# Scores and weighted sums of a pair's two heads issued in turns, one head on each half of the matmul array

## Chip, cores, metric

One core of a Trainium2 chip. The metric is device time in microseconds (us) of one execution of the whole program, lower is better. With one core there is no second die to compare, so a run is called fast if it lies within 1.5% of the fastest of its kernel.

PE is TensorE's matmul side, PEld its weight loads, DVE VectorE, ACT ScalarE, POOL GpSimd. "L157" is line 157 of the kernel in question; lines differ between kernels. A record is one line of the trace; an fp32 product leaves two (the eight score products of two heads are 16 records). The granted clock is the share of TensorE's full clock in the trace's clock records: there it is 1.0 or 0.5 and changes only on a grid of 3.413 us (788 records before, all but the last of whole multiples); records of 128x512 (L122 before) start 429 ns apart at 1.0 and 853 at 0.5 (medians). One step of this grid is called a stretch below.

## The reference, cut to what matters

Two images of 512 channels and 64 x 64 pixels go through four residual layers. Three of the four have attention over 8 heads of 64 channels, against 256 keys or features:

```python
# layer 0: 256 pooled keys and a 3 x 3 window in one softmax, plus learned window weights
attn_pool = jnp.einsum('bhnd,bhpd->bhnp', q_scaled, _l2norm(k_pool))
attn = jax.nn.softmax(jnp.concatenate([attn_local, attn_pool], axis=-1), axis=-1)
x_pool = jnp.einsum('bhnp,bhpd->bhnd', a_pool, v_pool)
# layer 1: 256 sampled keys
sim = jnp.einsum('bhid,bhjd->bhij', qh, kh)
out = jnp.einsum('bhij,bhjd->bhid', jax.nn.softmax(sim, axis=-1), vh)
# layer 3: 256 random features of keys and queries
data_dash = jnp.einsum('bhnd,md->bhnm', data * normalizer, proj)
context = jnp.einsum('bhnm,bhnd->bhmd', kp, v)
out = jnp.einsum('bhnm,bhmd->bhnd', qp, context) / denom[..., None]
```

Layer 2 (a choice of max pools) is not touched.

## The kernel before: what the change and the argument touch

Two heads share the 128 partitions of a channel chunk, so a head's scores contract over 64 rows and a head's weighted sum fills 64 output columns: `64*128` and `128*64` in the trace, where a full product (L122) is `128*128`, so half of the rows and half of the columns. A block is 512 tokens, a "pair" below is two heads of one block: 32 pairs per stage and image ("batch").

```python
def scores(self, pS, q, keys, h):
    lo = h * HD
    for t in range(NT):
        self.nc.tensor.matmul(pS[:, t, :], q[lo:lo + HD, t * P:(t + 1) * P],
                              keys[lo:lo + HD, :], start=True, stop=True)

def weighted(self, psO, prob, vals, h, sp, pp):
    pTs = []
    for k2 in range(2):
        pT = sp.tile([P, TB], F32, name="pT", bufs=2)
        # ... four transposes of prob into PSUM, copied to pT by ACT (k2 = 0) or DVE (k2 = 1)
    for k2 in range(2):
        nc.tensor.matmul(psO[h * HD:(h + 1) * HD, :], vals[:, k2, :], pTs[k2],
                         start=(k2 == 0), stop=(k2 == 1))

# layer 0, attend(blk); prepare(blk + 1) is issued in turn with it, a step at each yield
for h in range(2):
    pS = pps.tile([P, NT, NK], F32, name="pS")          # two such score tiles in PSUM
    self.scores(pS, qs, own["kp"], h)
    # ... maxima (DVE), yield, exp (ACT), normalisation (DVE), yield
    self.weighted(psO, prob, own["vp"][:, :, h * HD:(h + 1) * HD], h, wp, pp)
    yield
# ... nine taps: matmul(ps, taps[:, k, :], lt), 18 rows; product with vx on DVE into prod
#     (3 buffers); sum over taps on POOL; the final sum on DVE

# layer 3, context: one head g after the other
    self.scores(pS, Y[:, g // 2, blk * TB:(blk + 1) * TB], proj, g % 2)
    # ... four exp on ACT into kf, + 1e-4 on DVE, four matmuls va^T kf into ps
```

Layer 1's attention, layer 3's keys (scores and a maximum only) and layer 3's queries have the same loop over `h`. The build puts the instructions of each engine into an order of its own within what the dependences allow.

## Time and profile before

| | us |
|---|---|
| median of 4 runs | 10126.5 (10124.7 to 10127.7) |
| layer 0 attention, one batch | 1889 |
| layer 1 attention | 767 |
| layer 3 keys / context / queries | 320 / 362 / 850 |
| everything else in a batch | about 870 |

The stage lengths in this document are read from each trace between the same marker instructions (for instance the first score of layer 1 and the first pooling instruction of layer 2); they hold the seams between stages too, and so differ by some us from the windows in the prediction. Batch 1 is given where nothing else is said. A batch takes half of the span, so what a stage loses counts twice in the time.

### The profile page before, as it was taken

The numbers are of one execution on the slowest core, as the hardware profiler recorded it, in microseconds if no ns is written. First come the engines' busy times: TensorE is split into PE (matmuls) and PEld (weight loads), VectorE is DVE, ScalarE is ACT, GpSimd is POOL, SyncE is SP. The second block draws the span as 40 slices with busy tenths as digits, with TensorE's granted clock in tenths as the row PEclk, the third lists the DMA queues.
The fourth block names the chain that finished last, engine by engine and source line by source line (L and its number), as shares of the span: only waits on it lengthen the run. The fifth ranks groups of instructions, "written<-read, shape, count | busy, mean of one in ns | idle before, by whom it ended". The sixth has DMA issues, their size and how long they took to land. (4 is left out here: it accounts for less than half of the span.)

```text
span 10124.4 us, 68201 instructions
## 1 busy us (share of the span) xinstructions
PE 8632.9 (85%) x25390; PEld 4059.3 (40%) x25390; DVE 4276.9 (42%) x7503; ACT 2048.9 (20%) x4873; POOL 1093.5 (11%) x1190
## 2 busy tenths in 40 slices
PE   7989898988786699888889898989888876998887
PEld 3333333344333255544443333333443332555443
DVE  3444444425334922244434444444352359222343
ACT  1111111105222101222211111111142221022222
POOL 0222222200000000000002222222000000100000
PEclk9878888889887889977788887887898888899877
DMA  1000000000000000100000000000000000000000
GB/s 46 0 4 0 3 0 0 0 22 1 0 0 9 1 0 5 38 9 13 9 15 0 4 0 4 0 0 0 22 1 0 0 9 1 0 5 5 13 9 13
DMA packets 34324, 66.76 MB, mean 7 GB/s; under 512 B 2532, under 2 KB 15076, under 8 KB 32970
## 3 DMA queue, kind: packets, MB, share of 16 engines
q1 hardware_dynamic: 33994, 62.40, 1.8%
q8 instruction: 202, 3.31, 0.1%
q14 instruction: 128, 1.05, 0.0%
HBM read 45.62 MB, written 16.78 MB: 6 GB/s over the span
## 5 line engine op out<-in xcount | busy, mean ns | idle before, releaser
L122 PE MATMUL mm<-big,w 128*128 128x512 f32 x2560 | 1371.4, 682 | 0.0
L122 PEld LDWEIGHTS mm<-big,w 128*128 128x128 f32 x2560 | 532.6, 221 | 727.4 <-issue 639.9
L449 POOL TENSOR_TENSOR acc<-acc,prod 128x512 f32<-128x512 f32 x512 | 663.4, 1296 | 1441.3 <-DVE prod L444 1392.6
L442 PE MATMUL mm<-lt,taps 18*128 18x512 f32 x1152 | 761.2, 804 | 0.0
L166 PE MATMUL mm<-cst,prob 128*128 128x128 f32 x2048 | 429.7, 370 | 273.0 <-DVE prob L524 247.9
L388 PE MATMUL mm<-prod,cst 128*18 128x512 f32 x1152 | 648.5, 713 | 0.0
L169 DVE COPY pT<-mm 128x512 f32<-128x512 f32 x384 | 265.5, 691 | 787.4 <-PE mm L166 787.4
L166 PEld LDWEIGHTS mm<-cst,prob 128*128 128x128 f32 x2048 | 342.7, 194 | 511.3 <-issue 508.7
L154 PE MATMUL pS<-proj,big 64*128 64x256 f32 x2048 | 459.4, 444 | 98.5 <-ACT big L772 49.9
L444 DVE TENSOR_TENSOR prod<-vx,mm 128x512 f32<-128x512 f32 x512 | 351.9, 687 | 443.9 <-PE mm L442 356.6
L384 DVE TENSOR_TENSOR prod<-qs,kx 128x512 f32<-128x512 f32 x576 | 443.2, 800 | 195.6 <-PE mm L388 194.3
L713 PE MATMUL acc<-big,dg 128*128 128x512 f32 x768 | 369.0, 639 | 136.3 <-DVE big L681 71.4
L171 ACT COPY pT<-mm 128x512 f32<-128x512 f32 x384 | 224.8, 585 | 1000.8 <-PE mm L166 1000.8
L681 DVE TENSOR_TENSOR big<-big 128x3968 f32<-128x3968 f32 x96 | 410.4, 4286 | 21.2 <-PE acc L713 18.3
L442 PEld LDWEIGHTS mm<-lt,taps 18*128 18x128 f32 x1152 | 241.4, 232 | 424.9 <-issue 245.9
L154 PEld LDWEIGHTS pS<-proj,big 64*128 64x128 f32 x2048 | 307.1, 211 | 242.4 <-ACT big L772 103.7
L166 PE MATMUL mm<-cst,qf 128*128 128x128 f32 x1024 | 207.1, 354 | 219.0 <-DVE qf L884 219.0
L420 ACT ACTIVATE prob<-pS,nm 128x256 f32<-128x256 f32 x512 | 235.8, 473 | 630.9 <-DVE nm L415 625.7
L173 PE MATMUL psO<-pT,ctxm 128*64 128x512 f32 x512 | 334.2, 788 | 33.0 <-ACT pT L171 33.0
L173 PE MATMUL psO<-pT,vals 128*64 128x512 f32 x512 | 361.7, 800 | 0.0
L516 DVE TENSOR_REDUCE nm<-pS 128x4 f32<-128x1024 f32 x128 | 150.7, 1219 | 480.8 <-PE pS L154 480.8
L154 PE MATMUL pS<-proj,q 64*128 64x256 f32 x1024 | 280.2, 522 | 53.4 <-ACT q L863 53.4
(267 smaller groups left out, 11377.5 us busy)
## 6 DMA issues: line engine op xcount, KB each, us to landing
big<-in_x SPq DMA_DIRECT2D x8, 2048.0 KB, 8.3
out<-big SPq DMA_DIRECT2D x16, 1024.0 KB, 4.1
w<-in_W_kv SPq DMA_DIRECT2D x16, 256.0 KB, 3.8
big<-in_w_kv SPq DMA_DIRECT2D x2, 2048.0 KB, 7.8
w_sr<-in_W_sr SPq DMA_DIRECT2D x2, 1024.0 KB
w<-in_W_q SPq DMA_DIRECT2D x8, 256.0 KB, 3.0
w_proj<-in_W_proj SPq DMA_DIRECT2D x2, 1024.0 KB, 5.4
big<-in_w_out SPq DMA_DIRECT2D x2, 1024.0 KB
```

The costliest lines, as they stand in the source:

```text
L122: self.nc.tensor.matmul(ps, w[:, kc, :], X[:, kc, blk * TB:(blk + 1) * TB], start=(kc == 0), stop=(kc == KC - 1))
L154: self.nc.tensor.matmul(pS[:, t, :], q[lo:lo + HD, t * P:(t + 1) * P], keys[lo:lo + HD, :], start=True, stop=True)
L166: nc.tensor.transpose(ps[:, t * P:(t + 1) * P], prob[:, t, k2 * P:(k2 + 1) * P], self.ident)
L169: nc.vector.tensor_copy(pT, ps)
L173: nc.tensor.matmul(psO[h * HD:(h + 1) * HD, :], vals[:, k2, :], pTs[k2], start=(k2 == 0), stop=(k2 == 1))
L384: nc.vector.tensor_tensor(pr.rearrange("p (y x) -> p y x", x=W), qs.rearrange("p (y x) -> p y x", x=W), kx[:, dy:dy + 8, dx:dx + W], ALU.mult)
L388: nc.tensor.matmul(ps[:18, :], self.cst[:, C_TAP + 8 - k:C_TAP + 26 - k], pr, start=(k == 0), stop=(k == 8))
L442: nc.tensor.matmul(ps, taps[:, k, :], lt, start=True, stop=True)
L444: nc.vector.tensor_tensor(pr.rearrange("p (y x) -> p y x", x=W), vx[:, dy:dy + 8, dx:dx + W], ps.rearrange("p (y x) -> p y x", x=W), ALU.mult)
L449: nc.gpsimd.tensor_tensor(acc, acc, pr, ALU.add)
L681: nc.vector.tensor_tensor(o, a, b, ALU.max)
L713: nc.tensor.matmul(accs[b], dg, p2[:, b * TB:(b + 1) * TB], start=(j == 1), stop=(j == 6))
```

## The change

Its intent: two matmuls that use different halves of the array can run at the same time. (In the trace before, the sixteen records of L606, which alternate between the column halves, take 1.95 us, and the sixteen of L833, which all have the same columns, 3.67.) So both heads' score tiles are taken at once and their matmuls alternate, and the weighted sums wait until both heads are transposed and then alternate too. What the diff comes to, without the comments that it also drops:

```diff
-    def scores(self, pS, q, keys, h):
-        lo = h * HD
-        for t in range(NT):
-            self.nc.tensor.matmul(pS[:, t, :], ...)
+    def scores(self, q, keys, pps):
+        pS = [pps.tile([P, NT, NK], F32, name="pS") for _ in range(2)]
+        for t in range(NT):
+            for h in range(2):
+                lo = h * HD
+                self.nc.tensor.matmul(pS[h][:, t, :], q[lo:lo + HD, t * P:(t + 1) * P],
+                                      keys[lo:lo + HD, :], start=True, stop=True)
+        return pS
-    def weighted(self, psO, prob, vals, h, sp, pp):
+    def turned(self, prob, sp, pp):              # the transposes and copies alone
-            pT = sp.tile([P, TB], F32, name="pT", bufs=2)
+            pT = sp.tile([P, TB], F32, name="pT", bufs=4)
+    def weighted(self, psO, pTs, vals):
+        for k2 in range(2):
+            for h in range(2):
+                self.nc.tensor.matmul(psO[h * HD:(h + 1) * HD, :], vals[h][:, k2, :],
+                                      pTs[h][k2], start=(k2 == 0), stop=(k2 == 1))
 # in the five stages: both = self.scores(...) ahead of the loop over h, pS = both[h];
 # in three: pTs.append(self.turned(...)) in the loop, self.weighted(...) after it
 # in layer 0 (to make room, and a step more):
-                pr = wp.tile([P, TB], F32, name="prod", bufs=3)      # twice, and loc
+                pr = wp.tile([P, TB], F32, name="prod", bufs=2)
-        re = sp.tile([P, 2 * NT, HD], F32, name="hn_re", bufs=1)
+        re = sp.tile([P, 2 * NT, HD], F32, name="hn_re", tag="sq", bufs=1)
-                self.weighted(psO, prob, own["vp"][...], h, wp, pp)
+                pTs.append(self.turned(prob, wp, pp))
                 yield
+            self.weighted(psO, pTs, [own["vp"][:, :, h * HD:(h + 1) * HD] for h in range(2)])
+            yield
```

More of the change, by code (lines that the diff above doesn't have):

```diff
@@ L147, in head_norm @@
         nc.vector.tensor_tensor(out, raw, src, ALU.mult)
-    def scores(self, pS, q, keys, h):
-        lo = h * HD
+    def scores(self, q, keys, pps):
+        pS = [pps.tile([P, NT, NK], F32, name="pS") for _ in range(2)]
         for t in range(NT):
-            self.nc.tensor.matmul(pS[:, t, :], q[lo:lo + HD, t * P:(t + 1) * P],
-                                  keys[lo:lo + HD, :], start=True, stop=True)
-    def weighted(self, psO, prob, vals, h, sp, pp):
+            for h in range(2):
[4 more added lines that the diff above has]
+    def turned(self, prob, sp, pp):
         nc = self.nc
@@ L171, in weighted @@
                 nc.scalar.copy(pT, ps)
+        return pTs
+    def weighted(self, psO, pTs, vals):
         for k2 in range(2):
-            nc.tensor.matmul(psO[h * HD:(h + 1) * HD, :], vals[:, k2, :], pTs[k2],
-                             start=(k2 == 0), stop=(k2 == 1))
+            for h in range(2):
+                self.nc.tensor.matmul(psO[h * HD:(h + 1) * HD, :], vals[h][:, k2, :], pTs[h][k2],
+                                      start=(k2 == 0), stop=(k2 == 1))
     def layer0(self, X, Y, sp_scale, tokT, d):
@@ L391, in prepare @@
                     yield
-            loc = wp.tile([18, TB], F32, name="loc", tag="prod", bufs=3)
+            loc = wp.tile([18, TB], F32, name="loc", tag="prod", bufs=2)
             nc.scalar.copy(loc, ps[:18, :])
@@ L406, in attend @@
             psO = ppo.tile([P, TB], F32, name="psO")
+            both = self.scores(qs, own["kp"], pps)
+            pTs = []
             for h in range(2):
-                pS = pps.tile([P, NT, NK], F32, name="pS")
-                self.scores(pS, qs, own["kp"], h)
+                pS = both[h]
                 lh = locT[:, :, 9 * h:9 * h + 9]
@@ L429, in attend @@
                 yield
-                self.weighted(psO, prob, own["vp"][:, :, h * HD:(h + 1) * HD], h, wp, pp)
+                pTs.append(self.turned(prob, wp, pp))
                 yield
+            self.weighted(psO, pTs, [own["vp"][:, :, h * HD:(h + 1) * HD] for h in range(2)])
+            yield
             ps = pp.tile([P, TB], F32, name="mm")
@@ L442, in attend @@
                 nc.tensor.matmul(ps, taps[:, k, :], lt, start=True, stop=True)
-                pr = acc if k == 0 else wp.tile([P, TB], F32, name="prod", bufs=3)
+                pr = acc if k == 0 else wp.tile([P, TB], F32, name="prod", bufs=2)
                 nc.vector.tensor_tensor(
@@ L511, in layer1 @@
                         psO = ppo.tile([P, TB], F32, name="psO")
+                        both = self.scores(q, keys[:, cc, :], pps)
+                        pTs = []
                         for h in range(2):
-                            pS = pps.tile([P, NT, NK], F32, name="pS")
-                            self.scores(pS, q, keys[:, cc, :], h)
+                            pS = both[h]
                             nm = wp.tile([P, NT], F32, name="nm")
@@ L524, in layer1 @@
                             nc.vector.tensor_tensor(prob, prob, bcast(sm, 2, NK), ALU.mult)
-                            lo = cc * P + h * HD
-                            self.weighted(psO, prob, vals[:, :, lo:lo + HD], h, wp, pp)
+                            pTs.append(self.turned(prob, wp, pp))
+                        self.weighted(psO, pTs, [vals[:, :, lo:lo + HD]
+                                                 for lo in (cc * P, cc * P + HD)])
                         nc.scalar.copy(att[:, cc, :], psO)
@@ L774, in feature_keys @@
                                 pp)
-                for h in range(2):
-                    pS = pps.tile([P, NT, NK], F32, name="pS")
-                    self.scores(pS, k, proj, h)
+                for h, pS in enumerate(self.scores(k, proj, pps)):
                     nc.vector.tensor_reduce(top[:, 2 * cc + h, blk:blk + 1], pS, AX.XY, ALU.max)
@@ L823, in context @@
             for g in range(NH):
-                pS = pps.tile([P, NT, NK], F32, name="pS")
-                self.scores(pS, Y[:, g // 2, blk * TB:(blk + 1) * TB], proj, g % 2)
+                if g % 2 == 0:
+                    both = self.scores(Y[:, g // 2, blk * TB:(blk + 1) * TB], proj, pps)
+                pS = both[g % 2]
                 kf = wp.tile([P, NT, NK], F32, name="kf", bufs=2)
@@ L866, in feature_queries @@
                 psO = ppo.tile([P, TB], F32, name="psO")
+                both = self.scores(q, proj, pps)
+                pTs = []
                 for h in range(2):
                     g = 2 * cc + h
-                    pS = pps.tile([P, NT, NK], F32, name="pS")
-                    self.scores(pS, q, proj, h)
+                    pS = both[h]
                     nm = wp.tile([P, NT], F32, name="nm")
@@ L885, in feature_queries @@
                                                 ALU.add, ALU.mult)
-                    self.weighted(psO, qf, ctxm[:, :, g, :], h, wp, pp)
+                    pTs.append(self.turned(qf, wp, pp))
+                self.weighted(psO, pTs, [ctxm[:, :, 2 * cc + h, :] for h in range(2)])
                 nc.scalar.copy(att[:, cc, :], psO)
```

## The prediction

> **What bounds the kernel now.** I read the page first, then the groups with shapes kept apart, then busy time by stage, then the tensor engine's instructions in order of time for single iterations.
>
> ```profile
> PE 8632.9 (85%) x25390; PEld 4059.3 (40%) x25390; DVE 4276.9 (42%) x7503; ACT 2048.9 (20%) x4873; POOL 1093.5 (11%) x1190
> ```
>
> PE leads, but a busy PE is not a PE at its peak. The groups show what the change can touch (each fp32 product is two records, so a pair of heads has 16 score records, L154, and 8 weighted-sum records, L173, per block of 512 tokens; below, a pair means that):
>
> ```profile
> L154 PE MATMUL pS<-kp,qs 64*128 64x256 f32 x1024 | 316.0, 424 | 0.0
> ...
> L833 PE MATMUL mm<-kf,va 128*65 128x256 f32 x1024 | 237.4, 382 | 4.8 <-DVE kf L830 4.8
> ...
> L154 PE MATMUL pS<-keys,q 64*128 64x256 f32 x1024 | 189.7, 389 | 49.9 <-ACT q L509 49.9
> ...
> L606 PE MATMUL acc<-wt,q_tok 128*64 128x256 f32 x1024 | 127.1, 394 | 35.6 <-DVE wt L603 35.4
> ```
>
> All four stream 256 columns. The busy time per record is 309 ns for layer 0's scores, 232 for L833, 185 for layer 1's scores, 124 for L606. L606 already alternates between the two column halves. So the next view is PE in order of time, around single iterations (first fence: the sampling loop; second: layer 3's context).
>
> ```profile
> 2401.03 1.95 PE L606 MATMUL acc<-wt,q_tok 128*64 128x256 f32 x16
> ```
>
> ```profile
> 4010.10 2.00 PE L154 MATMUL pS<-proj,big 64*128 64x256 f32 x12
> ...
> 4013.94 3.67 PE L833 MATMUL mm<-kf,va 128*65 128x256 f32 x16
> ```
>
> Sixteen in turns take 1.95 us, sixteen not in turns 3.67: turns are worth almost a factor of two. But twelve scores, issued as four of one head and then eight of the other, take 2.00 us, which is eight slots of some 0.215: PE lets the second head start beside the first already, where nothing stands between them. A part of the gain is thus taken before the change.
>
> The stages of the first batch (layer 0's attention, layer 1's, layer 3's keys, context, queries):
>
> ```profile
> 174.00:2039.00 1865.00, 1692.09 (x4480) 695.15 (x4480) 834.48 (x1541) 323.74 (x909) 469.94 (x512) 0.82 0.01 2
> 2455.00:3218.00 763.00, 614.08 (x1813) 287.30 (x1812) 232.93 (x290) 201.05 (x643) 0.00 (x0) 0.86 0.00 0
> 3562.00:3890.00 328.00, 301.50 (x1034) 173.32 (x1035) 84.47 (x103) 21.54 (x32) 33.25 (x32) 0.83 0.01 4
> 3890.00:4248.00 358.00, 331.34 (x1298) 187.24 (x1296) 94.33 (x163) 100.68 (x268) 0.94 (x6) 0.99 0.07 27
> 4262.00:5059.00 797.00, 644.64 (x2015) 323.07 (x2016) 326.36 (x1086) 178.43 (x384) 33.25 (x32) 0.78 0.03 10
> ```
>
> Together 4111 of a batch's 5062 us; each has 32 pairs, so 58.3, 23.8, 10.3, 11.2 and 24.9 us per pair. The column after POOL is the granted clock: every stage but context runs a fifth to a third of its time at half speed. One layer 1 iteration in stretches of 3.41 us shows how:
>
> ```profile
> 2817.00:2820.41 3.41, 2.63 (x16) 2.32 (x16) 0.52 (x1) 0.69 (x1) 0.00 (x0) 1.00 0.00 0
> 2820.42:2823.83 3.41, 0.40 (x2) 0.00 (x0) 2.51 (x4) 2.69 (x12) 0.00 (x0) 1.00 0.00 0
> 2823.83:2827.24 3.41, 2.55 (x9) 1.85 (x10) 2.69 (x4) 1.66 (x7) 0.00 (x0) 0.50 0.02 5
> 2827.24:2830.65 3.41, 3.41 (x8) 1.00 (x6) 0.12 (x1) 0.59 (x1) 0.00 (x0) 0.50 0.00 0
> 2830.66:2834.07 3.41, 3.41 (x10) 1.10 (x10) 0.69 (x1) 0.00 (x0) 0.00 (x0) 1.00 0.01 2
> ```
>
> PE idles in the second stretch (scores done, softmax running), is at half speed in the next two, and whole again after a full one. I counted over all clock records of this trace: a stretch is followed by full speed if it streamed at least about 1.2 us (as at full speed) of products, each weighted by the rows that it fills. Iterations lock to these stretches: layer 1's is 20.5 us (6), layer 0's 54.6 in the steady state (16), two of the keys' 20.5.
>
> [...] the change gives each head its own pS, but thereby uses both score buffers for one pair.
>
> **The change part by part**, per pair. The order of the built program matters, so I compared both builds.
>
> *Context*: h1 t0-1, then h0/h1 in turn, where before it was h0 then h1. PE already overlapped them: eight slots before and after, and the chain (h0 scores 1.16, exponentials 1.5, next half scores 1.06, L833 3.6 = 7.44 us) is the same. 0.
>
> *Keys*: before: four records of h0, the norms (L799, held to 1.1 us after the scores' start by POOL's square, 1.04), then four pairs and four alone. After: two pairs, the norms, six pairs. Twelve slots become eight, but two of those hide behind POOL: 2 x 0.215 = 0.43. Six paired slots also count fully to the clock where four lone ones counted half, so I give one half-speed stretch (1.7 us) back in about half of the pairs: -1.3 per pair, -42 per batch.
>
> *Layer 1*: scores: h0 is done 2.0 us after the start before, 2.2 after, as all are paired; h1's earlier end is worth nothing, since the two maxima run one after the other on DVE (2.35 for both) anyway. +0.2. Then PE waits for exp and normalisation: transposes begin 7.0 us after the scores' start either way. From there, before: transposes of h0 1.9, four separate blocks of weighted sums and eight transposes up to 2834.7, that is 10 us, of it L536's first two 1.1. After: 16 transposes 3.6, then two pairs (1.4 half in the slow clock, 0.95), the projection of the next pair 3.5, 0.94 until its scores: 7.0 + 3.6 + 2.35 + 3.5 + 0.94 = 17.4, with 0.1 of gaps 17.5, against 20.5. Locking makes it 17.1 or 20.5, mixed. I take -2.75: -88 per batch.
>
> *Layer 3 queries*: the built DVE order is maximum h0, maximum h1, subtract, subtract. Before it was maximum, subtract, maximum; exp of h0 thus starts 1.2 (L872, 1.23) + 0.3 later, and one further L879 pass precedes the reciprocal: transposes at 10.7 instead of 8.4. The four weighted sums are h0 alone, three transposes and a projection in between, then three: six slots instead of eight, and h1's transposes no longer wait. I get 22.0 against (22.9 + 21.3 + 22.9 + 35.0 - 13.75)/4 = 22.1 from the four iterations of a block. 0.
>
> *Layer 0*, by far the longest, gains on PE and loses on waits. Gains: scores 16 records, 4.6 us, to ten slots, 2.4; weighted sums 4.2 to 3.0; 3.4 us at full speed. Losses: (a) An added yield moves the nine tap products (L442, 18 rows, so next to nothing for the clock) behind all nine local-score products; before, they were mixed with three of them. Now six taps stand together, most at half: 6 x 1.71. From the first tap to the last (three at full speed 2.85, scores 1.0, wait and transposes 1.25, six slow 10.3; now and then one more at full speed) it is 15 us. (b) Both maxima now stand on DVE behind the last tap, POOL's last addition and the final sum. The chain from the last tap: DVE 0.32 + 0.69, POOL 1.36, sum 0.7, two maxima 2.5, small ones and gap 0.3, three exp 1.45, then the projection's two copies (after its eight records) 1.4 to 2.1, exp 0.5, L423 twice 0.5, five small DVE 1.1, normalisation 1.25: 12 to 12.6 us until the transposes. Before it was 8.6, and normalisation was done long before PE came to it:
>
> ```profile
> 813.76 8.63 PE L122 MATMUL mm<-big,w 128*128 128x512 f32 x16
> ...
> 817.63 1.22 DVE L428 TENSOR_TENSOR prob<-prob,sm 128x1024 f32<-128x1024 f32 x1
> ...
> 822.22 1.04 PE L166 MATMUL mm<-cst,prob 128*128 128x128 f32 x8
> ```
>
> PE came at 822.2, the data was there at 818.85: 3.4 us of slack, which 4 us more use up. (c) Two prod buffers instead of three, one of them also for loc, which then waits for POOL: 0.9, and 0.07 per product. (d) The fillers between the head norm's steps are gone: 1.6 us idle, and the clock falls there. Sum: taps 15, chain 12.3, from h0's transposes to h1's 14.6 + 2.2 (projection at half speed), to the local scores 4.3, these 9.8: 58.2 against 54.6. On the lock that is 17 stretches, 58.0. About 30 of 32 pairs: +3.4 x 30 = +100 per batch; a lock at 16 would make it 0, so I weigh it to +75.
>
> Sum per batch: 75 - 88 - 42 + 0 + 0 = -55, twice -110: 10128 - 110, about 10020.
>
> **Rivals.** *The pairing pays in full*: 8 x 0.215 of scores in five stages of 32 pairs, and 4 x 0.45 of sums in three: 275 + 173 = 448 us per batch, 9230 in all. For it speaks L606; against it the pairing present already, DVE/ACT chains that PE waits for, and both score buffers bound to one pair. *Layer 0 keeps its 16 stretches*, the rest as above: 9870. *Layer 0 loses a stretch and layer 1 stays locked at six*: some 10250.
>
> **Range and chances.** Layer 0 decides: one stretch per pair is 3.4 x 64 = 218 us, 2.2%. Layer 1's lock is worth as much. So 9750 to 10290 for 8 in 10; faster by over 2% (below 9925) 0.28, within 0.59, slower 0.13.
>
> **What would show it.** Right: score and sum groups' busy time per record falls towards 120 and 240 ns; context unchanged; queries' exp 1.5 us later; in layer 0 an idle PE before L170, ended by DVE's prob; iterations still at multiples of 3.41. Wrong: a layer 0 iteration at or under 54.6; a clock share that rises in layer 0; weighted sums of a pair that do not overlap.

The limit of about 1.2 us comes from a count over the trace before. Counted again, with each record's work spread evenly over its time: with the limit at 1.26 us it is wrong for 4 of 2950 stretches, at 1.20 for 64; with the records of 18 rows counted as full height, for 254; PE's busy time instead, with its best limit, is wrong for 501. That iterations lock is read from their lengths alone (layer 1 before, within the last six of eight blocks: 20.42 to 20.47 us).

## The result, and the profile after

| | before | after |
|---|---|---|
| median of 4 runs, us | 10126.5 | 9940.6 (9935.8 to 9945.6) |
| ratio | | 0.982, 95% interval 0.980 to 0.983 |
| layer 0 attention | 1889 | 1891 |
| layer 1 attention | 767 | 661 |
| layer 3 keys / context / queries | 320 / 362 / 850 | 291 / 411 / 843 |

The ratios here and below are made from all fast runs of a round, so not quite the ratios of the medians. All outputs are right. The change saves 1.8%: just within 2%, and within the predicted range. The stages explain it: 2 - 105 - 29 + 49 - 7 = -90 us in a batch, twice -180, of 186 measured.

Busy time first (line of the page, after). PE lost 615 us of busy time and the span only 182:

```profile
PE 8018.2 (81%) x25390; PEld 3864.6 (39%) x25390; DVE 4180.9 (42%) x7503; ACT 2039.6 (21%) x4873; POOL 1077.6 (11%) x1190
```

The five stages of the first batch after (length; busy time of PE, weight loads, DVE, ACT, POOL; granted clock; DMA), in the order of the prediction's list:

```profile
172.00:2041.00 1869.00, 1614.79 (x4480) 682.12 (x4480) 794.87 (x1540) 322.77 (x909) 461.82 (x512) 0.81 0.01 2
2458.00:3116.00 658.00, 474.20 (x1811) 264.81 (x1810) 232.38 (x290) 200.99 (x643) 0.00 (x0) 0.85 0.00 0
3459.00:3762.00 303.00, 261.93 (x1032) 143.68 (x1033) 83.40 (x104) 21.64 (x32) 33.30 (x32) 0.85 0.01 4
3766.00:4166.00 400.00, 358.76 (x1294) 199.76 (x1293) 93.97 (x161) 100.40 (x268) 0.94 (x6) 0.92 0.07 24
4179.50:4970.00 790.50, 564.84 (x2012) 278.45 (x2013) 319.62 (x1085) 175.22 (x384) 33.30 (x32) 0.80 0.03 10
```

Three things stand out. Layer 0 has 77 us less PE work and nearly the same length. Layer 1 loses 105 us, with 140 us less PE work. And the context stage, in which the change should do nothing, is longer, busier, and has a lower clock: 0.92 where it had 0.99.

Layer 1 shows what the change is for. PE in order of time, an iteration before (columns: start, length, what; in brackets the idle time before it and what ended it):

```profile
2817.86 2.96 PE L154 MATMUL pS<-keys,q 64*128 64x256 f32 x16 [0.78 <-ACT q L509]
2824.69 1.94 PE L166 MATMUL mm<-cst,prob 128*128 128x128 f32 x8 [3.87 <-DVE prob L524]
2826.56 1.97 PE L173 MATMUL psO<-pT,vals 128*64 128x512 f32 x2
...
2833.71 1.07 PE L173 MATMUL psO<-pT,vals 128*64 128x512 f32 x2
```

and after:

```profile
2740.64 2.00 PE L157 MATMUL pS<-keys,q 64*128 64x256 f32 x16 [0.78 <-ACT q L522]
2747.54 3.76 PE L170 MATMUL mm<-cst,prob 128*128 128x128 f32 x16 [4.90 <-DVE prob L538]
2751.23 2.05 PE L183 MATMUL psO<-pT,vals 128*64 128x512 f32 x8
2753.21 3.70 PE L122 MATMUL mm<-big,wq 128*128 128x512 f32 x8
2757.69 2.00 PE L157 MATMUL pS<-keys,q 64*128 64x256 f32 x16 [0.78 <-ACT q L522]
```

The sixteen score records take 2.00 us instead of 2.96, and this does not bring the transposes forward, which start 6.9 us after the scores either way (6.83 before): PE's idle time before them grew from 3.87 to 4.90. (That the scores in turns gain something here all the same, behind the transposes, is seen in e1.) The eight sum records in turns take 2.05 us in one piece; before they stood in four pieces of 1 to 2 us between the transposes. The iteration is 17.05 us instead of 20.5: five stretches of 3.41 us instead of six.

Layer 0 after (answers to the fence at the end of the prediction's layer 0 part):

```profile
800.30 3.02 PE L455 MATMUL mm<-lt,taps 18*128 18x512 f32 x6
...
805.35 10.06 PE L455 MATMUL mm<-lt,taps 18*128 18x512 f32 x12
...
818.19 7.79 PE L122 MATMUL mm<-big,w 128*128 128x512 f32 x16
826.58 1.06 PE L170 MATMUL mm<-cst,prob 128*128 128x128 f32 x8 [0.59 <-DVE prob L439]
...
831.43 3.60 PE L122 MATMUL mm<-big,w 128*128 128x512 f32 x8
...
840.80 1.91 PE L170 MATMUL mm<-cst,prob 128*128 128x128 f32 x8
...
854.88 3.02 PE L455 MATMUL mm<-lt,taps 18*128 18x512 f32 x6
```

The taps stand together, twelve of the eighteen records largely at half speed (10.06 us, granted clock 0.53), and the transposes now wait for DVE's `prob`, both as predicted; but the iteration, from 800.30 to the same instruction of the next at 854.88, is still 54.6 us.

The context stage, PE in order of time. Before, the wait ahead of a pair's last four score records was this (the twelve ahead of it and the sixteen sum records behind it are in the prediction, 2.00 and 3.67 us):

```profile
4012.89 1.13 PE L154 MATMUL pS<-proj,big 64*128 64x256 f32 x4 [0.78 <-ACT kf L828]
```

After, two pairs:

```profile
3936.91 1.99 PE L157 MATMUL pS<-proj,big 64*128 64x256 f32 x12
3940.15 1.13 PE L157 MATMUL pS<-proj,big 64*128 64x256 f32 x4 [1.24 <-ACT kf L842]
3941.21 3.67 PE L847 MATMUL mm<-kf,va 128*65 128x256 f32 x16
3944.80 1.99 PE L157 MATMUL pS<-proj,big 64*128 64x256 f32 x12
3948.04 1.13 PE L157 MATMUL pS<-proj,big 64*128 64x256 f32 x4 [1.24 <-ACT kf L842]
3949.10 5.36 PE L847 MATMUL mm<-kf,va 128*65 128x256 f32 x16
```

Twelve score records take 2 us before and after, as predicted. But in turns, the first head's last scores come later among them: the first exponential starts 1.62 us after the scores (3938.53) where it started 1.16 after them (4011.26), and the wait is 1.24 instead of 0.78. That is 0.46 us a pair, 15 us a batch. The larger part is in the last line: the same sixteen sum records take 5.36 us in more than half of the pairs. Their stretch of 3.41 us is at half clock; the one before held little PE work, 2.16 us busy, most of it half-height scores (length, busy times, then granted clock):

```profile
3905.20:3908.61 3.41, 2.16 (x11) 1.26 (x9) 0.69 (x1) 2.97 (x8) 0.00 (x0) 1.00 0.00 0
3908.62:3912.02 3.40, 3.40 (x10) 1.83 (x9) 0.94 (x2) 0.05 (x1) 0.00 (x0) 0.50 0.02 5
```

That this is what counts can be checked on the whole trace of the changed kernel. Take the time that a matmul's columns need at full clock (0.216 us for 256 columns, from one start of such records to the next), multiply it by the share of the 128 rows that it fills, and add this up in each stretch: the first stretch above has 1.00 us, the second 1.73. A limit of 1.25 us on this sum says of all but 38 of 2898 stretches whether the next one is at full speed; the best limit on PE's busy time is wrong for 501, the best limit on the longest gap for 536.

Of 64 such groups of sixteen in both batches, 38 take over 5 us after; before, none of the groups does. 19 a batch, each 1.69 us longer, are 32 us. 15 + 32 = 47, of 49 measured.

In the queries, DVE takes both maxima before it subtracts, as predicted, and the first exponential starts on average 6.7 us after the first score instead of 5.3. Lines of DVE and ACT of one pair, after (its first score stands at 4445.71, so here it is 7.5):

```profile
4450.69 2.35 DVE L887 TENSOR_REDUCE nm<-pS 128x4 f32<-128x1024 f32 x2 [2.61 <-PE pS L157]
4452.97 0.28 DVE L888 TENSOR_TENSOR nm<-nm,dq 128x4 f32<-128x4 f32 x2
4453.21 3.03 ACT L892 ACTIVATE qf<-pS,nm 128x256 f32<-128x256 f32 x8 [7.56 <-DVE nm L888]
```

### The profile page after: what moved, and what is told of

Read it like the earlier page. It is cut to its first block, busy times and chain, and to the rows that moved or that the text cites. A ratio compares the mean times of both kernels' runs of the same rounds, so it can differ in the third digit from the quotient of the medians.

```text
span 9942.8 us, 67989 instructions
## 1 busy us (share of the span) xinstructions
PE 8018.2 (81%) x25390; PEld 3864.6 (39%) x25390; DVE 4180.9 (42%) x7503; ACT 2039.6 (21%) x4873; POOL 1077.6 (11%) x1190
## 5 line engine op out<-in xcount | busy, mean ns | idle before, releaser
L122 PE MATMUL mm<-big,w 128*128 128x512 f32 x2560 | 1295.9, 653 | 0.0
L455 PE MATMUL mm<-lt,taps 18*128 18x512 f32 x1152 | 830.1, 883 | 2.6 <-DVE lt L449 1.5
L122 PEld LDWEIGHTS mm<-big,w 128*128 128x128 f32 x2560 | 518.8, 214 | 662.2 <-issue 648.6
L398 PE MATMUL mm<-prod,cst 128*18 128x512 f32 x1152 | 552.1, 604 | 0.0
L157 PE MATMUL pS<-proj,big 64*128 64x256 f32 x2048 | 398.8, 460 | 130.5 <-ACT kf L842 78.0
L394 DVE TENSOR_TENSOR prod<-qs,kx 128x512 f32<-128x512 f32 x576 | 391.4, 690 | 228.4 <-PE mm L398 228.1
L455 PEld LDWEIGHTS mm<-lt,taps 18*128 18x128 f32 x1152 | 290.0, 263 | 445.5 <-issue 396.7
L696 DVE TENSOR_TENSOR big<-big 128x3968 f32<-128x3968 f32 x96 | 410.4, 4285 | 20.3 <-PE acc L728 17.4
L170 PEld LDWEIGHTS mm<-cst,qf 128*128 128x128 f32 x1024 | 172.7, 198 | 529.4 <-issue 391.1
L141 PE MATMUL mm<-cst,hn_re 128*128 128x128 f32 x528 | 122.0, 373 | 302.6 <-DVE hn_re L138 208.5
L157 PEld LDWEIGHTS pS<-proj,big 64*128 64x128 f32 x2048 | 252.3, 212 | 268.8 <-ACT big L787 103.7
L842 ACT ACTIVATE kf<-pS,diag 128x256 f32<-128x256 f32 x512 | 193.9, 490 | 621.7 <-PE pS L157 621.7
```

The costliest lines, as they stand in the source:

```text
L122: self.nc.tensor.matmul(ps, w[:, kc, :], X[:, kc, blk * TB:(blk + 1) * TB], start=(kc == 0), stop=(kc == KC - 1))
L157: self.nc.tensor.matmul(pS[h][:, t, :], q[lo:lo + HD, t * P:(t + 1) * P], keys[lo:lo + HD, :], start=True, stop=True)
L170: nc.tensor.transpose(ps[:, t * P:(t + 1) * P], prob[:, t, k2 * P:(k2 + 1) * P], self.ident)
L394: nc.vector.tensor_tensor(pr.rearrange("p (y x) -> p y x", x=W), qs.rearrange("p (y x) -> p y x", x=W), kx[:, dy:dy + 8, dx:dx + W], ALU.mult)
L398: nc.tensor.matmul(ps[:18, :], self.cst[:, C_TAP + 8 - k:C_TAP + 26 - k], pr, start=(k == 0), stop=(k == 8))
L455: nc.tensor.matmul(ps, taps[:, k, :], lt, start=True, stop=True)
```

## The experiments

Twelve kernels. First each half of the change alone, and single stages undone.

**e1: scores in turns, sums as before.** Against the changed kernel:

```diff
-                pTs.append(self.turned(prob, wp, pp))
+                self.weighted_one(psO, self.turned(prob, wp, pp, 2), vals_of_h, h)
-            self.weighted(psO, pTs, [...])
 # in layer 0, 1 and the queries; buffers and steps of layer 0 as before the change
```

> Scores in turns everywhere, weighted sums, yields and buffers as before. Theory (scores in turns win only in layer 3's keys, -25 us per batch, lose in context, +42, and delay the queries' first exp): 10128 + 2 x (42 - 25 + some 10 to 40 in the queries) = 10180 to 10240, slower than before. Rival (each half of the change brings half of the gain of 186 us): about 10035.

Measured 10135.5 us (10125.9 to 10138.4), ratio to before 1.001 (0.999 to 1.002). Both expectations missed, the total is that of before. By stages against before: layer 0 -12, layer 1 -34, keys -29, context +48, queries +23 (batch 2: +37). The theory had left out layers 0 and 1. In layer 1 the transposes start as late as before (6.83 us), but the last sum stands 15.4 us after the scores instead of 16.3, and the half-clock share of the stage is 0.25 instead of 0.29: the gain seems to come with the clock; no run tests this alone.

**e2: sums in turns, scores head by head.**

```diff
-            both = self.scores(qs, own["kp"], pps)
 ...
-                pS = both[h]
+                pS = pps.tile([P, NT, NK], F32, name="pS")
+                self.score_one(pS, qs, own["kp"], h)
 # in all five stages
```

> Weighted sums in turns everywhere (with the change's buffers and its added step in layer 0), scores head by head. Theory: layer 1 keeps nearly all of its -105 us per batch (17.1 us per iteration), context and keys are as before, the queries gain 30 to 60 as exp of the first head starts 1.2 us earlier than in the changed kernel; layer 0 within one clock stretch per pair either way: 9830 to 9870, faster than the changed kernel. Rival (half of the gain): about 10035.

Measured 9967.5 us (9964.9 to 9969.5), ratio 0.984 (0.983 to 0.986): between the two expectations, so both miss. By stages against before: layer 0 +33, layer 1 -70, keys and context 0, queries -45. In layer 0, 32 of 62 iterations take 58.0 us, the 17 stretches that the prediction had given for the whole change:

```profile
829.87 1.10 PE L187 MATMUL mm<-cst,prob 128*128 128x128 f32 x8
...
877.09 9.86 PE L122 MATMUL mm<-big,w 128*128 128x512 f32 x16
...
887.94 1.09 PE L187 MATMUL mm<-cst,prob 128*128 128x128 f32 x8
```

So the two halves do different things in each stage. Keys gain and context loses by the scores alone. Layer 1's 105 is 34 + 70, from both. The queries' -7 is a gain of 45 from the sums and a loss from the scores that nearly eats it: two effects, where the prediction had none of either. In layer 0 the sums with their smaller buffers and later step cost 33, and the scores in turns buy that back: one stretch lost and one won.

**e3: the change without the context's scores in turns.**

> The changed kernel with only context's scores head by head again. Theory (the turns' order there delays the first head by 0.46 us and makes the clock fall): context back from 400 to 358 us per batch, 9940 - 84 = 9856. Rival (context is slower for what it inherits, or by chance of the clock's phase): context stays near 400, 9940.

```diff
-                if g % 2 == 0:
-                    both = self.scores(Y[:, g // 2, ...], proj, pps)
-                pS = both[g % 2]
+                pS = pps.tile([P, NT, NK], F32, name="pS")
+                self.score_one(pS, Y[:, g // 2, ...], proj, g % 2)
```

Measured 9858.0 us (9850.1 to 9861.8), ratio 0.974 (0.972 to 0.975). The context stage is back at 367 (362 before), and no group of sixteen is slow (of the groups of eight, which the order head by head has too, two are). The context's scores in turns cost 83 us, as the theory had it, and without them the change is 2.6% faster than the kernel before.

**e4: the change without layer 0's part.**

> The changed kernel with all of layer 0 as before (order, steps, buffers). Theory (layer 0's iteration locks to 16 clock stretches with and without the change, so the change is worth nothing there): 9940 within 20. Rival 1 (turns gain 3.4 us per pair in layer 0 and the change's own buffers and waits take them back, with net zero by chance): also 9940, told apart by the traces alone. Rival 2 (layer 0 does gain, another stage loses in the whole): over 9990.

Layer 0's scores, sums, buffers and steps are those of before. Measured 9942.2 us (9941.7 to 9943.0), ratio 0.982; layer 0 1888 against 1891. As expected, all of the change in layer 0 together is worth nothing. This total fits the theory and rival 1 alike; the stretch that e2 loses and the whole change does not speaks for rival 1, a loss and a gain that cancel.

**e5 and e6: is it the clock in the context?** If the clock goes by how much the stretch before streamed, then useless work in the idle 1.2 us should make the stage shorter. And if it goes by rows in use, the same work on 18 rows should not. Against the changed kernel, one matmul for each pair, written where the sums' `start=True` overwrites it (that PSUM tile is therefore taken earlier, in both runs alike):

```diff
+                if fill and t == NT - 1 and h == 1:     # rows: 128 in e5, 18 in e6
+                    self.nc.tensor.matmul(ps_of_sums, self.ident[:rows, :],
+                                          self.cst[:rows, :TB], start=True, stop=True)
```

> The changed kernel with one useless matmul (128 rows of the identity against 512 columns of constants, 0.86 us at full clock, into a PSUM tile that the sums overwrite) for each pair of heads in the context stage, issued just before the two scores that wait for the exponentials. The changed kernel idles 1.24 us there, and its x16 sums then run at half clock in about half of the pairs (5.36 us instead of 3.67). Theory (the clock of a stretch of 3.41 us follows how much row-weighted matmul work it held): the extra work lifts every stretch over the threshold, the sums go back to 3.67 us, the context stage gets shorter although it does more: from 400 to 365 us in a batch, the whole from 9941 to about 9870, the granted clock of the stage from 0.92 to 0.98 or more. Rival (the loss in the context stage is only the later exponentials of the first head, the clock follows from it and not the other way round): the stage stays at 400 or grows by up to 28 us in a batch, the whole is 9940 to 9995.

> The same as e5 with the extra matmul on 18 rows instead of 128: the same number of instructions, the same columns, the same place, and the same time on PE. Theory (rows count for the clock): 18 rows are a seventh of the work, the stretches stay under the threshold, the stage stays at 400 us in a batch or grows, the whole is 9940 to 9995, 70 us or more above e5. Rival 1 (the clock follows the time for which PE is busy, whatever the rows): the same time as e5 within 10 us. Rival 2 (clock has nothing to do with it): both runs 9940 to 9995.

Measured: e5 9880.4 us (9873.5 to 9885.1), ratio 0.976 (0.974 to 0.977); e6 9923.3 us (9915.3 to 9925.8), ratio 0.980 (0.978 to 0.981). The context stage: 411 in the changed kernel, 381 in e5, 397 in e6 (batch 2: 400). PE in e5:

```profile
3963.59 1.56 PE L160 MATMUL pS<-proj,big 64*128 64x256 f32 x10
3965.08 1.12 PE L157 MATMUL mm<-cst 128*128 128x512 f32 x2
3966.14 1.81 PE L160 MATMUL pS<-proj,big 64*128 64x256 f32 x6
3967.89 3.67 PE L870 MATMUL mm<-kf,va 128*65 128x256 f32 x16
```

and in e6:

```profile
3971.17 5.35 PE L870 MATMUL mm<-kf,va 128*65 128x256 f32 x16
3976.46 1.56 PE L160 MATMUL pS<-proj,big 64*128 64x256 f32 x10
3977.95 1.12 PE L157 MATMUL mm<-cst 18*128 18x512 f32 x2
3979.00 1.82 PE L160 MATMUL pS<-proj,big 64*128 64x256 f32 x6
```

The extra matmul takes the same 1.12 us in both and closes PE's gap in both. With 128 rows all 64 groups of sums take 3.67 us; with 18 rows 24 of 64 still take 5.1 to 5.4. So more work made the stage 30 us shorter, and the rows of the matmul matter, not the time for which PE is busy: that is shown. e5 came out near its theory (9870; the stage 30 us shorter, 35 said) and its rival is out; both rivals of e6 are out. My own expectation for e6 was still missed: I had said that 18 rows help not at all, and they took 38 slow groups to 24. The count of stretches, made on e6's trace, says that such a matmul counts for its rows: with a weight of 18/128 it is wrong for 39 of 2891 stretches, with 0 for 79, with 1 for 311. That the shifted issue also moved some pairs on the 3.41 us grid is not excluded.

**e7: the same question in layer 0.** Its tap matmuls have 18 rows and take 10.06 us for twelve records in the changed kernel. Rows of zeros make them 128 high:

```diff
-                taps = wp.tile([18, 9, P], F32, name="taps", bufs=1)
-                nc.sync.dma_start(taps, d["taps"])
+                taps = wp.tile([P, 9, P], F32, name="taps", bufs=1)     # zeroed once
+                nc.sync.dma_start(taps[:18], d["taps"])
+                self.lt2 = wp.tile([P, 2, TB], F32, name="lt2", bufs=1) # zeroed once
-            lt = wp.tile([18, TB], F32, name="lt")
+            lt = self.lt2[:, blk % 2, :]       # rows 0 to 17 written as before
```

> The changed kernel with layer 0's tap matmuls (18 rows of weights against 512 columns, 18 records per pair of heads) made 128 rows high by rows of zeros: same results, same count, no more time at one clock. In the changed kernel 4 of the 5 half-clock stretches of a layer 0 iteration (16 stretches, 54.6 us) fall on these taps. Theory (rows count for the clock): the 4 stretches turn to full clock, the taps go from 713 ns to about 460 ns a record, the iteration locks at 14 or 15 stretches (47.8 or 51.2 us), layer 0's attention goes from 1869 to 1650 to 1760 us in a batch, the whole from 9941 to 9500 to 9720. Rival 1 (the clock follows busy time, not rows): nothing changes, 9930 to 9950. Rival 2 (layer 0 is held by the chain over DVE and POOL, whatever PE's clock): the taps get faster, PE idles instead, and the whole stays above 9900.

Measured 9904.8 us (9897.4 to 9914.5), ratio 0.978 (0.977 to 0.980); layer 0 1867 against 1891. PE:

```profile
816.18 1.94 PE L187 MATMUL mm<-cst,prob 128*128 128x128 f32 x8 [4.55 <-DVE prob L459]
...
852.35 5.42 PE L475 MATMUL mm<-lt,taps 128*128 128x512 f32 x12
```

Half of the theory came true: twelve tap records take 5.42 us instead of 10.06, on average 476 ns of busy time a record instead of 721, and the clock's part of the theory is shown a second time, in another stage (granted clock 0.86, 0.81 in the changed kernel). The other half did not: the iteration stays near 54.6 us and the whole above 9720. What PE gained it now idles (11.2 us a pair instead of 7.9), and the half clock moved to the place behind that wait: 86 of 100 transposes of batch 1 start at half speed, 52 in the changed kernel. This fits rival 2: layer 0 is held by the loop over DVE, ACT and POOL (exponentials, normalisation, transposes, products, taps, sums), in which PE's taps are only one link. How much of that loop is the half clock behind the wait is left to e11.

**e8: context's and queries' scores head by head, and filling matmuls in layer 1.** Four matmuls of 128 rows before the first head's transposes:

```diff
+            for _ in range(warm if k2 == 0 else 0):     # warm = 4 for the first head
+                nc.tensor.matmul(ps, self.ident, self.cst[:, :TB], start=True, stop=True)
             for t in range(NT):
                 nc.tensor.transpose(ps[:, t * P:(t + 1) * P], ...)
```

> The changed kernel with the scores of the context and of the queries head by head again (sums still in turns, keys and layers 0 and 1 as changed), and four useless full-height matmuls per pair of heads of layer 1 before the first head's transposes, where PE idles 4.90 us. Stages are read one by one. From runs e2 and e3, context and queries should take 42 and 38 us less in a batch than in the changed kernel: 9780 without the layer 1 part. Layer 1, theory: half-clock stretches vanish (granted clock 0.85 to 0.95 or more) and the iteration falls from 17.07 to 13.7 to 15.5 us, the stage from 658 to 560 to 620 us in a batch, so 9630 to 9740 in all. Rival (layer 1 is held by the chain scores, maximum, exponentials, product, transposes, and the extra 3.4 us only fills the wait): stage 658 within 5 us, 9780 in all; or the extra matmuls delay the scores and it grows.

Measured 9774.3 us (9773.5 to 9777.7), ratio 0.965 (0.964 to 0.967). Context 367 and queries 803, as the earlier runs said. The queries, same view as for the changed kernel:

```profile
4346.90 1.22 DVE L905 TENSOR_REDUCE nm<-pS 128x4 f32<-128x1024 f32 x1 [0.89 <-PE pS L170]
4348.16 0.16 DVE L906 TENSOR_TENSOR nm<-nm,dq 128x4 f32<-128x4 f32 x1
4348.24 1.22 DVE L905 TENSOR_REDUCE nm<-pS 128x4 f32<-128x1024 f32 x1
4348.42 1.56 ACT L910 ACTIVATE qf<-pS,nm 128x256 f32<-128x256 f32 x4 [4.84 <-DVE nm L906]
```

Head by head, DVE takes a maximum, subtracts, and only then takes the second, and ACT starts 4.8 us after the first score. All but the block ends are now 20.5 us, where the changed kernel has 21.1 and 22.8.

Layer 1 stayed at 661, although its granted clock rose from 0.85 to 0.97. The filling did what it should to the clock and nothing to the time: the rival's 9780 came true, the theory's 560 to 620 for the stage did not. PE:

```profile
2733.49 2.00 PE L157 MATMUL pS<-keys,q 64*128 64x256 f32 x16
2735.42 2.84 PE L187 MATMUL mm<-cst 128*128 128x512 f32 x6
2740.38 1.06 PE L189 MATMUL mm<-cst,prob 128*128 128x128 f32 x8 [2.13 <-DVE prob L557]
2741.69 1.07 PE L202 MATMUL psO<-pT,vals 128*64 128x512 f32 x2 [0.24 <-ACT pT L194]
2742.69 1.09 PE L189 MATMUL mm<-cst,prob 128*128 128x128 f32 x8
```

The transposes are faster (1.06 for eight), but the build moved the first two sum records ahead of the second head's transposes, away from their partners (1.07 + 1.93 us instead of 2.05), and one filling matmul ahead of the scores. Iterations of 16.6 and 17.9 us mix to about the same 17.05: three in a row take 51.05 us in 7 of 8 blocks, 51.12 in the changed kernel, 15 stretches both. Whether filling alone would have helped there is open: the order changed with it.

**e9 to e12: the parts put together.** e9 is e8 without layer 1's filling and with e7's taps. e10 is e9 with layer 0's sums and buffers as before the change (scores stay in turns). e11 is e9 with three filling matmuls before the first head's transposes in layer 0. e12 has both. The edits are those shown above.

> Scores of the context and of the queries head by head, sums in turns, layer 0's taps on 128 rows, no filling matmuls. If the parts add up by stages: context and queries 42 and 40 us less in a batch than the changed kernel (from e3 and e8), layer 0 24 less (e7), so 9941 - 2 x 106 = 9730, 9715 to 9745; about 0.961 of the kernel before. Rival (parts do not add, because each stage's clock depends on where the 3.41 us grid falls): above 9760.

> As e9, with layer 0's sums head by head and its buffers as before (scores in turns stay). From e1 (layer 0 at 1877 instead of 1889) against the changed kernel (1889 to 1891), the buffers and the step cost layer 0 about 12 us in a batch: 9705 if that adds to the taps' gain, 9730 (as e9) if not. Theory of the prediction's layer 0 step (fewer product buffers and the later sums lengthen the chain behind the taps): at least 20 us below e9.

> As e9, with three useless full-height matmuls (2.6 us at full clock) before the first head's transposes in layer 0, where PE idles 4.55 us in e7 and the transposes then run at half clock (86 of 100 records). Theory (layer 0 is held by a chain in which these half-clock transposes stand; an iteration of 54.6 us is 16 stretches): the transposes go from 1.94 to about 1.1 us, the iteration falls by 1 to 3.4 us, layer 0 by 30 to 110 us in a batch: 9510 to 9670. Rival (the chain over DVE, ACT and POOL alone holds the iteration, and filling only moves the half-clock stretches elsewhere): 9715 to 9750, as e9.

> e10 with the three filling matmuls of e11 before the first head's transposes in layer 0. If both gains are of different parts (e10: shorter chain by the product buffers and the sums, 20 us in a batch; e11: transposes at full clock, 31 to 34 us in a batch) they add: 9620, 9600 to 9640. If both only buy back the same half-clock stretches, the two overlap: 9650 to 9690, not below e11.

| | us | ratio to before | layer 0, batch 1 / 2 | most iterations of layer 0 |
|---|---|---|---|---|
| e9 | 9728.7 (9720.0 to 9732.8) | 0.961 (0.959 to 0.962) | 1864 / 1865 | 54.6 to 57 |
| e10 | 9689.5 (9687.1 to 9698.9) | 0.957 (0.956 to 0.958) | 1850 / 1844 | 54.3 to 54.9 |
| e11 | 9657.8 (9655.3 to 9663.4) | 0.954 (0.952 to 0.955) | 1833 / 1830 | 51.6 to 55.7 |
| e12 | 9577.8 (9575.6 to 9579.1) | 0.946 (0.944 to 0.947) | 1791 / 1787 | 51.2 to 52.2 |

e9 is where the sum of the parts said (9730). e10 is 39 us faster, more than expected (9705 at best): layer 0's smaller buffers and later sums do cost time, some 18 us a batch, as the prediction's step says in kind (I had put 20 us in all as the least that would show it). e11 gained 33 us a batch by doing useless work, at the upper end of its expected time: of 100 transposes in layer 0, 49 start at half clock instead of 86, so the rival (filling only moves the half clock) is out. e12 missed both of its expectations on the good side (9600 to 9640, 9650 to 9690): the two gains, 18 and 33, gave 75 together. PE in e12:

```profile
841.47 2.74 PE L187 MATMUL mm<-cst 128*128 128x512 f32 x6
845.29 1.06 PE L189 MATMUL mm<-cst,prob 128*128 128x128 f32 x8 [1.08 <-DVE prob L461]
```

Its iterations stand at 51.2 us, which is 15.0 stretches of 3.413, where those of before and of the change stand at 54.6, 16.0 of them. The tap gain of e7, less than a stretch, had shown only in part; the savings together make up a whole stretch and show in full. This fits the prediction's picture of iterations that lock to the grid of the clock, but the lock itself was not tested by a run of its own, and the queries of the changed kernel (21.1 and 22.8 us) do not show it. It can also span several iterations: in e1 and e2 the single iterations of layer 1 (18.5 to 19.9 and 17.4 to 19.1 us within a block) are no multiples of 3.413, but three in a row take 57.95 and 54.55 us in 7 of 8 blocks, 17 and 16 stretches. e12 is 5.4% faster than the kernel before and 3.6% faster than the changed one.

## Why the prediction was right or wrong

The total was 0.8% off and in the range (10020 said, 9941 measured). It was closer than its steps were, which is in part luck: the context's loss (+49 a batch, 0 said) hides most of what layer 0 was wrong by (0, +75 said).

- **"PE overlapped them" and the size of the gain on PE**: right. Of the twelve score records before, four of one head and then eight of the other, the first eight start in pairs 13 ns apart and then four alone, 2.00 us in all. Layer 1's scores go from 185 to 125 ns a record and its sums from 706 to 263, near the 120 and 240 that were named as signs; layer 0's go only from 309 to 259 and from 535 to 408. The full-pay rival (9230) assumed that this PE time is time; PE's busy time fell by 615 us and the span by 182.
- **Context, 0**: wrong, and the one step that failed in kind. +49 a batch, of which the scores alone are the cause (e3). "The same chain" failed (its four terms add up to 7.32 us, and the 7.44 is the pair's measured interval; after, it is 7.89 even with fast sums): the first head is ready 0.46 us later when its partner is served in between, and the step did not put this stage to the count of stretches that the prediction had just stated. The stage stood at 0.99, so it was taken for safe; with 0.46 us more of waiting it stands at 0.92. Over the trace after, the same count is wrong for 21 of 2897 stretches with its best limit, 1.30 us; the longest gap of PE in the stretch, with its best limit, is wrong for 536. With e5's useless work the stage is 30 of the 49 shorter (411 to 381).
- **Keys, -42**: right in kind, -29 measured. The size failed in the term for the clock, one half-speed stretch given back in about half of the pairs, -1.3 us with the 0.43 of slots: the iteration fell by 0.9 us on average, and only every third or fourth is a short one (8.1 us among 9.8).
- **Layer 1, -88**: the gain is 105. Nearly all iterations within a block stand at five stretches (17.05), where I had weighed five against six.
- **Queries, 0**: -7, right for a wrong reason. The later exponential was predicted at 1.5 us and came to 1.4 (5.3 to 6.7 us), but the transposes, said to start at 10.7 us instead of 8.4, start at 9.9 instead of 8.8 (medians). And the sums in turns alone are worth 45 (e2), and the step saw them as no more than two slots that even this out. A zero made of +38 and -45 is a thing to be taken apart, not to be left.
- **Layer 0, +75**: 0 measured (e4). The step's own sum was 15 + 12.3 + 16.8 + 4.3 + 9.8 = 58.2. In the lines after, the first tap stands at 800.3, the last ends at 815.4, transposes start at 826.6 and 840.8, local scores at 845.0, the next tap at 854.9: 15.1 + 11.2 + 14.2 + 4.2 + 9.9 = 54.6. Four of the five terms hold within 1.1 us (the chain is the one that is 1.1 shorter). The one that failed is the third, 14.2 for 16.8, in its "2.2 (projection at half speed)": L122 x8 at 831.43 takes 3.60 us, full speed (granted clock 1.00). The idle time that was to bring the half clock is there (1.54 us before the head norm's second part, L141), the half clock is not. The idle time before the transposes is 0.59 us, as 4 us more against 3.4 us of slack should give. The sign of being wrong that was named, an iteration at or under 54.6, came true. The 58.0 of e2 does not rescue the step: there the same projection is at full speed too (3.60 us), and the time is lost elsewhere, for instance in the sixteen records of the next one (9.86 us, 7.79 in the changed kernel). The chance of a lock at 16 was named, and given too little weight.
- **Rivals**: "layer 0 keeps its 16 stretches, 9870" was the closest in mechanism; the context's loss of 49 a batch, 98 in all, separates it from the 9941 measured, less some 27 us of smaller misses in other stages.
- **One reading of the lines** was too low: "a fifth to a third of its time at half speed". Granted clocks of 0.82, 0.86, 0.83 and 0.78, made of 1.0 and 0.5, mean 36, 28, 34 and 44%. No step of the sum used it.

## What to carry to other kernels

Where two instructions already overlap because they stand next to each other, alternating them further can give PE nothing (context: 2.00 us for twelve score records before, 1.99 after) and can delay the first consumer (by 0.46 us there); alternate where something stands between them (here the weighted sums, with transposes between), and leave head by head where a chain starts from the first head. Ask of every stage, above all of one at full clock, how far it stands from the edge at which the clock falls (in the two traces, by count, some 1.26 to 1.30 us of row-weighted streaming in the stretch before): in the context, a wait longer by 0.46 us a pair, 15 us a batch, came with a stage 49 us longer. Where PE idles anyway, a useless full-height matmul, or rows of zeros, can be cheaper than the half clock that comes with the idle time or the few rows (33 us a batch less in e11, 24 in e7); but look at what the build's order makes of it.
